# Cross attention and experts on one core: weights transposed by VectorE and moved through DRAM instead of transposed by TensorE

## The chip, the core and the metric

The kernel runs on one core of one Trainium2 chip. TensorE (PE; its weight loads are listed as PEld) multiplies from on-chip memory (SBUF) into accumulators (PSUM[...]); VectorE (DVE), ScalarE (ACT) and GpSimd (POOL) do the rest; SyncE (SP) issues most DMAs between SBUF and the chip's DRAM. The engines run their own instruction lists in order and wait for each other by semaphores. The metric is the device time of one execution in microseconds (us), lower being better.

## The reference

```python
# x (4,1024,256); ctx (4,77,256); fside (4,16); 16 heads of 64
def _L0_xattn_ref(x, latents, shift, scale, ...):
    xn = layernorm(x, ln1_w, ln1_b);  ln = layernorm(latents, ln2_w, ln2_b)
    q = ln @ Wq;  k, v = jnp.split(xn @ Wkv, 2, axis=-1)
    q = q * (1.0 + scale[:, None, :, None]) + shift[:, None, :, None]
    qk = jnp.einsum('bihd,bjhd->bhij', q, k) * DIM_HEAD ** (-0.5)
    out = jnp.einsum('bhij,bjhd->bihd', jax.nn.softmax(qk, axis=-1), v)
    return out.reshape(b, -1, INNER) @ Wout

x = x + _L0_xattn_ref(ctx, _layernorm(x), fside, fside, ...)
x = x + _L0_ffn_ref(_layernorm(x), Wr, Wg, Wu, Wd)   # 9 experts of width 704, top 2, silu gate
```

The call passes the 77 context rows as `x` and the 4,096 tokens as `latents`: each token asks 77 keys in each of 16 heads. The second part routes each token to two of nine experts. All is float32.

## The kernel before

Tokens are taken in 8 groups of 512 (`NG`), and a group in 4 sub-blocks of 128 (`NS`): 32 sub-blocks in all, numbered i. The key, query and output matrices are folded beforehand: `g_sb[b]` gives the scores of a normalised token against all 16 x 77 head-keys of batch b in one product, and `u_sb[b]` takes the 1,232 softmax weights of a token straight to its 256 outputs and 9 router logits (`DE` = 265). A batch has two groups. The weights of 64 keys per head fill 8 chunks of 128 rows, the remaining 13 keys of each head two more: `KC` = 10 chunks.

One sub-block goes through these steps:

- `query` (L241, VectorE) normalises the tokens, `query_turn` (L250, TensorE, then a ScalarE copy) turns them.
- `scores` (L263) makes three PSUM banks of 462, 462 and 317 columns, each with one buffer, and VectorE takes each head's negative maximum (L267).
- `exponentials` (L277) runs one ScalarE instruction per head, 16 in all, into `ex`; `queries_logits` (L288) takes the router's share.
- `attention_weights`: VectorE sums `ex` (L297), inverts (L299), and multiplies into `an` (L301 and L305), which has two buffers.
- `weights_turn` (L313 to L319): TensorE transposes the ten chunks of `an` into three PSUM tiles, so that keys lie on partitions; `weights_copy` (L321 to L327): ScalarE copies these to `aT`.
- `values` (L336): ten products of `aT` with `u_sb` (in the profile two matrix instructions each); `attended` (L344, L345) adds the result to x and to the logits; `residual_stats` (L351) prepares the second norm.

The order is written out by hand in the loop from L1434 (the kernel runs under a manual schedule, so each engine gets its instructions in program order). Iteration i holds the scores and exponentials of sub-block i, and the transposes, copies and values of sub-block i - 1. On TensorE the order is scores, weight transposes, query transposes of i + 1, values. Routing of group g - 1 (second norm, logits, top two, places in the experts' lists) is spread over the same iterations as short VectorE instructions; SP writes `out` (L847) and `y_d` (L881) once per group and loads x two groups ahead (L204).

Ahead of the loop, context products fill `g_sb` and `u_sb`. `fill` (L793) makes parts of `u_sb` (16 parts, batch by chunk pair); the other 13 keys' part, `urem`, is placed in `u_sb` by 32 small SBUF-to-SBUF DMAs (L769).

After the loop come the expert blocks: six "early" ones (256 tokens of one expert), whose lists rest on the first five groups, and then pairs, single units and mixed ones, whose lists need all groups. The routing of the last group and the tables of these late blocks (`late_blocks`, L1054) are handed out by `pump` (L1369), `STEP` = 6 steps after each of a block's six hidden tiles (L1242); when the steps are used up, `fetch` issues on POOL the gathers of the late blocks' row lists (`ids`, L1183) and rows (`yin`, L1183). Block j's `turn` (L1228, TensorE) is put behind block j - 1's hidden tiles; then comes `down` (L1320) of the block before, whose result `adding` (L1355, POOL) adds to the output.

Of the kernel before, what the change touches and what calls it, by code (L numbers as in the profile page):

```python
# [8 lines left out]
F32 = mybir.dt.float32  # L9
# [12 lines left out]
def kernel(  # L22
# [76 lines left out]
    y_d = dram.tile([TOK, D], F32, name="y_d")  # L99
    list_d = dram.tile([ROWS, 2], I32, name="list_d")  # L100
# [88 lines left out]
    def open_attention():  # L189
        for name, bufs in (("xpool", 3), ("qpool", 2), ("rpool", 2)):  # L190
            pools[name] = attention.enter_context(tc.tile_pool(name=name, bufs=bufs, side="right"))
        q = pools["qpool"]
        zs.extend(q.tile([P, D], F32, name=f"z{i}", bufs=1) for i in range(2))
        an_of.extend(q.tile([P, NA], F32, name=f"an{i}", bufs=1) for i in range(2))
        for z in zs:
            nc.gpsimd.memset(z[:, D - 1 : D], 1.0)
        for an in an_of:
            nc.gpsimd.memset(an[:, H * JA :], 0.0)
# [14 lines left out]
    def query_variance(g):  # L213

        st = zstats.pop(g)
        mv = stat.tile([P, NS, 2], F32, tag="mvq", name=f"mv_q{g}", bufs=2)
# [18 lines left out]
    zTs, exs, ans, lgs, aTs, nmx, fstats, pscs = {}, {}, {}, {}, {}, {}, {}, {}  # L235
# [36 lines left out]
    def exponentials(i, k):  # L272
        h, n = banks[k]
        if k == 0:
            exs[i] = pools["qpool"].tile([P, H, J], F32, tag="ex", name=f"ex{i}")
        for q in range(n):
            nc.scalar.activation(  # L277
                exs[i][:, h + q, :], pscs[k][:, q * J : (q + 1) * J], AF.Exp,
                bias=nmx[i][:, h + q : h + q + 1],
            )  # L280
# [12 lines left out]
    def attention_weights(i):  # L293

        ex = exs.pop(i)
        sm = stat.tile([P, H], F32, tag="sm", name=f"sm{i}")
        nc.vector.tensor_reduce(sm, ex, AX.X, ALU.add)  # L297
        rs = stat.tile([P, H], F32, tag="rs", name=f"rs{i}")
        nc.vector.reciprocal(rs, sm)  # L299
        an = ans[i] = an_of[i % 2]  # L300
# [3 lines left out]
        )  # L304
        nc.vector.tensor_tensor(  # L305
            an[:, H * JA :].rearrange("p (h w) -> p h w", w=W)[:, :, :JR], ex[:, :, JA:J],
            rs.unsqueeze(2).to_broadcast([P, H, JR]), ALU.mult,
        )

    TURNS = [(k, min(4, KC - k)) for k in range(0, KC, 4)]  # L310
    pas = {}

    def weights_turn(i):  # L313
        for k, m in TURNS:
            pa = pas[k] = mm_tile(f"pa{i}_{k}")
            for q in range(m):
                nc.tensor.transpose(  # L317
                    pa[:, q * P : (q + 1) * P], ans[i][:, (k + q) * P : (k + q + 1) * P], ident
                )  # L319

    def weights_copy(i, t):  # L321
        if t == 0:
            aTs[i] = pools["qpool"].tile([P, KC, P], F32, tag="aT", name=f"aT{i}")
        k, m = TURNS[t]
        nc.scalar.copy(  # L325
            aTs[i][:, k : k + m, :].rearrange("p k t -> p (k t)"), pas[k][:, : m * P]
        )  # L327

    pos = {}

    def values(i):
        b = i // NS // GPB
        aT = aTs.pop(i)
        po = pos[i] = mm_tile(f"po{i}")
        for n in range(KC):
            nc.tensor.matmul(  # L336
                po[:, :DE], aT[:, n, :], u_sb[b][:, n, :], start=(n == 0), stop=(n == KC - 1)
# [18 lines left out]
    with ExitStack() as kvs:  # L356
# [247 lines left out]
        for i in range(2):  # L604
            nc.gpsimd.memset(u_half[i][:, :, NP:, :], 0.0)
# [158 lines left out]

        def other_keys_placed(b):
            for k in range(2):
                for q in range(2 * N2 // NR):
                    at = (2 * q + k) * W
                    nc.sync.dma_start(  # L769
                        out=u_sb[b][at : at + JR, NP:, :],  # L770
                        in_=urem[64 * k + b * W : 64 * k + b * W + JR].rearrange(
                            "p (r q) d -> p r q d", r=NR
                        )[:, :, q, :],
                    )

        EARLY_V = 5
        QB = TB // P
        for n in range(EARLY_V):
            if n < 2:
                for c in range(C):  # L780
                    turn_wo(n * QB, c)
            elif n == 3:
                wo_logits()
            context_values(n)
            if n == 3:
                for q in range(NS):
                    query_stats(0, q)
                query_variance(0)
                query_root(0)
                query_scale(0)  # L790
        turn_logits()
# [5 lines left out]

        context_values(EARLY_V)
        fill((0, 0), (1, 0), (2, 0), (3, 0), new=bank_tile)

        nc.scalar.activation(junk, eps_t, AF.Exp)
        context_values(EARLY_V + 1)
        fill((0, 1), (1, 1), new=bank_tile)
        context_values(EARLY_V + 2)
        for n in range(N2):
            other_keys(n)
        for b in range(B):
            other_keys_placed(b)
        query(0)
        fill((0, 2), (1, 2))  # L810
        query_turn(0)
        query(1)
        fill((0, 3), (1, 3))
        for k in range(len(banks)):
            scores(0, k)
            exponentials(0, k)
            if k == 0:
                fill((2, 1), (3, 1))
                query_turn(1)
            else:  # L820
                fill((1 + k, 2))
    left = [(2, 3), (3, 3)]
# [322 lines left out]
    def weights(j):  # L1145
# [9 lines left out]
        load(tabs[kind][0][0:1, at : at + 1], w, downs[j][0])  # L1155

    def weights_upper(j):

        _, i, kind = blocks[j]
        if kind == "flex":  # L1160
            load(tabs[kind][0][0:1, 2 * i + 1 : 2 * i + 2], late["w2"], late["d2"])

    def load(number, w, d):
# [5 lines left out]
        nc.sync.dma_start(out=w[:, :, 0:FF], in_=wg_v)  # L1169
        nc.sync.dma_start(out=w[:, :, FF : FF + FT], in_=wu_v[:, :, NF * P :])  # L1170
        nc.sync.dma_start(out=w[:, :, FF + FT : FF + FB], in_=wu_v[:, :, FA : NF * P])
        nc.sync.dma_start(out=w[:, :, FF + FB :], in_=wu_v[:, :, 0:FA])
        nc.sync.dma_start(
# [5 lines left out]
        )  # L1179

# [26 lines left out]

    Q = 32
# [157 lines left out]
    STEP, HOLD = 6, 3  # L1366
# [20 lines left out]
    def fetch():  # L1387

        end = NBLK if late_ready() else EARLY
        for name, fn, lead in (  # L1390
# [8 lines left out]
            while ahead[name] < min(now[0] + lead + 1, end):  # L1399
                fn(ahead[name])  # L1400
# [31 lines left out]
    N_SUB = NG * NS  # L1432
    chosen, early = None, None
    for i in range(N_SUB + 1):  # L1434
        g, s = divmod(i, NS)
        now_on = i < N_SUB
        q = g - 1

        if now_on:
            if i:  # L1440
                scores(i, 0)
                if i < 3:
                    fill(left[i - 1])
                exponentials(i, 0)
            if i > 1:
                residual_stats(i - 2)
            if i:
                scores(i, 1)
            if 0 < i < N_SUB - 1:
                query(i + 1)  # L1450
            if i:
                scores(i, 2)
        if i:
            weights_turn(i - 1)
            weights_copy(i - 1, 0)
            weights_copy(i - 1, 1)
        if i == 2:
            vsides.close()
        if now_on and i:
            exponentials(i, 1)  # L1460
        if 0 < i < N_SUB - 1:
            query_turn(i + 1)
        if now_on and i:
            exponentials(i, 2)
        if i:
            weights_copy(i - 1, 2)
        if now_on:
            queries_logits(i)
            if s == 1 and q > 0:
                ranks(q - 1)  # L1470
            if i == (G_EARLY + 1) * NS + 2:
                early = early_blocks()
                advance(early, 2)
        else:
            turn(0)
            advance(chosen)
            ranks(q - 1)
            residual_stats(i - 2)
        if i:
            values(i - 1)  # L1480


        if now_on and s == 0:
            if g + 1 < NG:
                for k in range(NS):
# [132 lines left out]
```

## Time and profile before

| what | us |
|---|---|
| median of 3 runs (lowest, highest) | 908.5 (907.83, 910.33) |
| the profiled execution's own time | 908.26 |
| its span in the trace | 906.6 |
| TensorE busy in the span | 890.6 (98%) |
| VectorE busy | 588.2 (65%) |
| ScalarE busy | 317.8 (35%) |
| GpSimd busy | 315.9 (35%) |
| preparation, up to the loop's first repeated part | 0 to 75.5 |
| sub-blocks | 75.5 to 388 |
| expert blocks | 388 to 906.6 |

The shares are averages over stages with different limits, so the table is only a start: VectorE's 65% says little about the sub-blocks, where it is busier than among the experts. In the page's groups a row reads: line, engine, operation, result<-operands, shapes, count | busy time in all, mean length of one in ns | idle time of the engine just ahead of it and what ended it. Instructions of one engine overlap, so busy time divided by the count can be well under the mean length. How long a step holds TensorE is read from the starts in the timeline.

The page's chain of waits covers only the last few us, DMAs of the final additions, so it isn't used here. The waits view of TensorE lists 8 causes of waiting, the largest 2.4 us (the first weights' arrival) and none of them repeated.

### The profile page before, as it was taken

What the parts mean: (1) busy time and instruction counts of PE and PEld (TensorE: products, weight loads), DVE (VectorE), ACT (ScalarE), POOL (GpSimd) and SP (SyncE); (2) the same over time, 40 slices, a digit from 0 to 9 for tenths busy, and PEclk for the clock granted to TensorE, in tenths of its full rate; (3) what the DMA queues carried; (4) which work ended last, traced back from release to release, by engine and by line L of the source; (5) the groups of instructions that cost most, each with busy time, mean ns of one, the idle gap of its engine ahead of it and who ended that gap; (6) DMA issues with size and microseconds to landing.
All of it is one profiled execution on the core that took longest, in us unless ns stands there. A gap on an engine that the chain in (4) does not pass through costs nothing. (4 is left out here: it accounts for less than half of the span.)

```text
span 906.6 us, 13816 instructions
## 1 busy us (share of the span) xinstructions
PE 890.6 (98%) x4184; PEld 684.0 (75%) x4184; DVE 588.2 (65%) x1854; ACT 317.8 (35%) x1021; POOL 315.9 (35%) x328
## 2 busy tenths in 40 slices
PE   8999999999999999999999999999999999999996
PEld 6656777777777777788887777777777777778885
DVE  5776688878888887753626666666665666665641
ACT  3566566565656566551211111111111111111110
POOL 3000002130504252146554445435435435444332
PEclk9999999999999999999999999999999999999998
DMA  7011010503202710456769779779879878779722
GB/s 266 3 21 43 24 47 25 47 25 47 66 28 48 227 36 24 120 145 183 184 193 301 214 221 305 221 218 303 242 212 317 229 216 229 221 224 321 235 30 23
DMA packets 110379, 137.94 MB, mean 152 GB/s; under 512 B 24664, under 2 KB 80288, under 8 KB 110305
## 3 DMA queue, kind: packets, MB, share of 16 engines
q1 hardware_dynamic: 92746, 119.66, 43.2%
q0 software_dynamic: 17344, 17.26, 10.1%
q8 instruction: 34, 0.56, 0.3%
q14 instruction: 41, 0.33, 0.2%
q10 hardware_dynamic: 214, 0.13, 0.0%
HBM read 119.48 MB, written 18.33 MB: 152 GB/s over the span
## 5 line engine op out<-in xcount | busy, mean ns | idle before, releaser
L1242 PE MATMUL pg<-xT,wgu 128*128 128x256 f32 x1144 | 251.7, 379 | 0.7 <-DVE xT L1215 0.7
L1242 PEld LDWEIGHTS pg<-xT,wgu 128*128 128x128 f32 x1144 | 215.9, 190 | 29.6 <-issue 1.1
L1320 PE MATMUL po<-wd,hid 128*128 128x256 f32 (+1 forms) x804 | 180.9, 380 | 0.0
L1320 PEld LDWEIGHTS po<-wd,hid 128*128 128x128 f32 (+1 forms) x804 | 149.2, 187 | 28.0 <-issue 3.7
L277 ACT ACTIVATE ex<-psc,mx 128x77 f32<-128x77 f32 x512 | 123.6, 360 | 100.1 <-DVE mx L267 98.8
L1215 DVE STREAM_TRANSPOSE xT<-yin 32x128 f32<-32x128 f32 (+1 forms) x544 | 148.4, 273 | 14.2 <-DMA yin<-y_d,ids 5.4
L1355 POOL DMA_INDIRECT out_dram<-co,ids x63 | 100.7, 1599 | 162.0 <-DVE co L1323 133.9
L950 POOL DMA_INDIRECT list_d<-r_entry,r_pli x64 | 69.0, 1078 | 247.3 <-issue 119.7
L336 PE MATMUL po<-u,aT 128*128 128x265 f32 x640 | 151.7, 391 | 0.5 <-ACT aT L325 0.2
L263 PE MATMUL psc<-g,zT 128*128 128x462 f32 (+1 forms) x384 | 139.7, 511 | 0.0
L336 PEld LDWEIGHTS po<-u,aT 128*128 128x128 f32 x640 | 118.7, 189 | 23.3 <-ACT aT L325 1.5
L1249 DVE TENSOR_TENSOR hid<-pg,sl 128x256 f32<-128x256 f32 x130 | 55.0, 424 | 121.8 <-ACT sl L1248 120.8
L1248 ACT ACTIVATE sl<-pg 128x256 f32<-128x256 f32 x130 | 49.7, 383 | 219.6 <-PE pg L1242 193.0
L263 PEld LDWEIGHTS psc<-g,zT 128*128 128x128 f32 x384 | 72.2, 189 | 58.2 <-issue 50.8
L1183 POOL DMA_INDIRECT yin<-y_d,ids x67 | 70.2, 1048 | 26.5 <-issue 18.9
L297 DVE TENSOR_REDUCE sm<-ex 128x16 f32<-128x1232 f32 x32 | 45.9, 1435 | 35.9 <-ACT ex L277 35.9
L267 DVE TENSOR_REDUCE mx<-psc 128x6 f32<-128x462 f32 (+1 forms) x96 | 55.7, 580 | 19.7 <-PE psc L263 16.9
L1323 DVE TENSOR_SCALAR co<-po,ids 128x256 f32<-128x256 f32 x67 | 32.3, 484 | 53.0 <-PE po L1320 51.4
L325 ACT COPY aT<-pa 128x512 f32<-128x512 f32 (+1 forms) x96 | 49.4, 552 | 27.7 <-PE pa L317 27.7
L317 PEld LDWEIGHTS pa<-ident,an 128*128 128x128 f32 x320 | 36.9, 141 | 7.7 <-PE po L336 1.4
L317 PE MATMUL pa<-ident,an 128*128 128x128 f32 x320 | 40.2, 273 | 1.0 <-DVE an L301 1.0
L301 DVE TENSOR_TENSOR an<-ex,rs 128x1024 f32<-128x1024 f32 x32 | 39.2, 1224 | 1.1
(312 smaller groups left out, 761.2 us busy)
## 6 DMA issues: line engine op xcount, KB each, us to landing
wgu<-in_L_ffn_Wg_dram SPq DMA_DIRECT2D x41, 704.0 KB
wd<-in_L_ffn_Wd_dram SPq DMA_DIRECT2D x41, 640.0 KB
wgu<-in_L_ffn_Wu_dram SPq DMA_DIRECT2D x41, 512.0 KB
wgu<-in_L_ffn_Wu_dram SPq DMA_DIRECT2D x41, 128.0 KB
x<-in_x_dram SPq DMA_DIRECT2D x8, 512.0 KB
out_dram<-x SPq DMA_DIRECT2D x8, 512.0 KB
y_d<-y SPq DMA_DIRECT2D x8, 512.0 KB
w<-in_L_ffn_Wg_dram SPq DMA_DIRECT2D x5, 704.0 KB
```

Of the source, the lines that this page charges most:

```text
L263: nc.tensor.matmul(psc[:, :w], zT[:, c, :], g_sb[i // NS // GPB][:, c, h * J : h * J + w], start=(c == 0), stop=(c == C - 1),)
L267: nc.vector.tensor_reduce(nmx[i][:, h : h + n], psc[:, : n * J].rearrange("p (h j) -> p h j", h=n), AX.X, ALU.max, negate=True,)
L277: nc.scalar.activation(exs[i][:, h + q, :], pscs[k][:, q * J : (q + 1) * J], AF.Exp, bias=nmx[i][:, h + q : h + q + 1],)
L317: nc.tensor.transpose(pa[:, q * P : (q + 1) * P], ans[i][:, (k + q) * P : (k + q + 1) * P], ident)
L336: nc.tensor.matmul(po[:, :DE], aT[:, n, :], u_sb[b][:, n, :], start=(n == 0), stop=(n == KC - 1))
L950: i = nc.gpsimd.indirect_dma_start(out=list_d[:, :], out_offset=bass.IndirectOffsetOnAxis(ap=place_i[:, s : s + 1], axis=0), in_=entries[k ...
L1183: return nc.gpsimd.indirect_dma_start(out=dst, out_offset=None, in_=src, in_offset=bass.IndirectOffsetOnAxis(ap=offsets, axis=0), **kw,)
L1215: yield nc.vector.transpose(xT[q : q + Q].rearrange("p c (h t) -> p h c t", t=P)[:, :nh, :, a : a + Q], of(yins, j)[a : a + Q].rearrange(" ...
L1242: nc.tensor.matmul(pg[:, g, :], w[:, c, at : at + P], xT[:, c, :], start=(c == 0), stop=(c == C - 1),)
L1249: nc.vector.tensor_tensor(hid[:, f, :], pg[:, 1, :], sl, ALU.mult)
L1320: nc.tensor.matmul(po[rows, :D], hid[:, f, at], d[:, f, :], start=(f == 0), stop=(f == NF))
L1355: i = nc.gpsimd.indirect_dma_start(out=out_r, out_offset=bass.IndirectOffsetOnAxis(ap=rows_of(j, h, rows), axis=0), in_=cos[j][:, h, :], i ...
```

## The change

The ten TensorE transposes and three ScalarE copies of each sub-block go. Instead VectorE transposes `an` in squares of 32 by 32 within each quarter of the partitions, one DMA writes the result to DRAM (`a_d`, two buffers), and four DMAs read it back with the keys of each chunk on their partitions. `aT` keeps two buffers; `an` and the transposed `anT` have one. Keys are numbered so that the four quarters fit (the second multiplication writes in another order; `u_sb`'s other keys go through a DRAM tile, `u_d`, in one write and eight reads). The exponentials give out their sums by `accum_out`, and the VectorE sum goes.

```diff
 def exponentials(i, k):
...
-                bias=nmx[i][:, h + q : h + q + 1],
+                bias=nmx[i][:, h + q : h + q + 1], accum_out=sms[i][:, h + q : h + q + 1],
...
 def attention_weights(i):
-        ex = exs.pop(i)
-        sm = stat.tile([P, H], F32, tag="sm", name=f"sm{i}")
-        nc.vector.tensor_reduce(sm, ex, AX.X, ALU.add)
+        ex, sm = exs.pop(i), sms.pop(i)
...
-        an = ans[i] = an_of[i % 2]
+        an = an_of[0]
...
     def weights_turn(i):
-        for k, m in TURNS:
-            pa = pas[k] = mm_tile(f"pa{i}_{k}")
-            for q in range(m):
-                nc.tensor.transpose(
-                    pa[:, q * P : (q + 1) * P], ans[i][:, (k + q) * P : (k + q + 1) * P], ident
-                )
...
-        nc.scalar.copy(
-            aTs[i][:, k : k + m, :].rearrange("p k t -> p (k t)"), pas[k][:, : m * P]
-        )
+        turned = pools["qpool"].tile([P, NQ, Q, KC], F32, tag="anT", name=f"anT{i}", bufs=1)
+        nc.vector.transpose(
+            turned.rearrange("p q t k -> p q k t"), an_of[0].rearrange("p (k q t) -> p q k t", q=NQ, t=Q)
+        )
+        aT = aTs[i] = pools["qpool"].tile([P, NQ, Q * KC], F32, tag="aT", name=f"aT{i}")
+        there = a_d[i % 2]
+        nc.sync.dma_start(out=there, in_=turned.rearrange("p q t k -> p (q t k)"))
+        by_key = there.rearrange("(a i) (q m) -> q i a m", i=Q, q=NQ)
+        for q in range(NQ):
+            nc.sync.dma_start(out=aT[q * Q : (q + 1) * Q], in_=by_key[q])
...
     def values(i):
...
-        aT = aTs.pop(i)
+        aT = aTs.pop(i).rearrange("p a (t k) -> p (a t) k", k=KC)
...
-                po[:, :DE], aT[:, n, :], u_sb[b][:, n, :], start=(n == 0), stop=(n == KC - 1)
+                po[:, :DE], aT[:, :, n], u_sb[b][:, n, :], start=(n == 0), stop=(n == KC - 1)
```

The loop is written anew. Iteration i holds the scores of i, the weights and their transposes of i - 1 and the values of i - 3 (`LAG` = 3); all that follows a group's values moves with them. Scores of sub-block 0 are made among the context products, and 12 of the 16 fills move into iterations 1 to 3. The expert weights of the first three blocks are issued in parts, between the DMAs of `aT`:

```diff
+            attention_weights(i - 1)
...
+            weights_turn(i - 1)
...
+            values(d)
...
-            if advance(early, 7):
+            if advance(early, 9):
                 early = None
                 now[0] = -1
-                fetch()
+                fetch(in_parts=True)
+        elif partly and advance(partly[0], 1):
+            partly.pop(0)
...
+    late_values(N_SUB - 2)
+    rest.append(listed_second_last())
+    in_first = {2: [last_values], 3: [lambda: turn(1)]}
...
-    STEP, HOLD = 6, 3
+    STEP, HOLD = 8, 3
```

The values of the last sub-block are put behind the third hidden tile of the first expert block, and the routing of the last two groups, not of one, is handed out by `pump`, 8 steps at a time. `load_x` keeps four groups in place of three. The other keys' placing:

```diff
+        def other_keys_there():
+            nc.sync.dma_start(out=u_d, in_=urem.rearrange("p n d -> p (n d)"))
...
-                for q in range(2 * N2 // NR):
-                    at = (2 * q + k) * W
-                    nc.sync.dma_start(
-                        out=u_sb[b][at : at + JR, NP:, :],
...
+                nc.sync.dma_start(
+                    out=u_sb[b][64 * k : 64 * k + 64, NP:, :],
+                    in_=rows[k, b].rearrange("p (t d) -> p t d", t=2),
+                )
```

Two memsets of `u_half` on POOL go with it.

## The prediction

> **What bounds the kernel now.** I read the busy times by stage first, then the order of TensorE's work inside one attention sub-block, then the costliest groups. The windows view (columns: length, then busy time and instructions of PE, PEld, DVE, ACT, POOL, then clock, DMA share, GB/s) gives for six groups of four sub-blocks and for the stage after them:
>
> ```profile
> 116.00:362.00 246.00, 245.73 (x1087) 179.75 (x1086) 201.76 (x600) 148.46 (x541) 62.40 (x76) 1.00 0.24 57
> 388.00:490.00 102.00, 101.58 (x482) 88.74 (x481) 50.62 (x201) 26.38 (x55) 55.60 (x54) 1.00 0.73 202
> ```
>
> TensorE has work in 245.7 of 246 us at a granted clock of 1.00: it is the bound. A sub-block lasts 246/24 = 10.25 us; VectorE is busy 201.76/24 = 8.41 of it, ScalarE 6.19. The timeline of TensorE shows what fills one:
>
> ```profile
> 206.64 4.33 PE L263 MATMUL psc<-g,zT 128*128 128x462 f32 x12
> 210.81 1.25 PE L317 MATMUL pa<-ident,an 128*128 128x128 f32 x10
> 211.90 0.38 PE L250 MATMUL pz<-ident,z 128*128 128x128 f32 x2
> 212.14 4.75 PE L336 MATMUL po<-u,aT 128*128 128x265 f32 x20
> ```
>
> From start to start: scores 4.17, weight transposes 1.09, query transposes 0.24, values (to 216.72, the next scores) 4.58. The page's groups price the rest:
>
> ```profile
> L277 ACT ACTIVATE ex<-psc,mx 128x77 f32<-128x77 f32 x512 | 123.6, 360 | 100.1 <-DVE mx L267 98.8
> L336 PEld LDWEIGHTS po<-u,aT 128*128 128x128 f32 x640 | 118.7, 189 | 23.3 <-ACT aT L325 1.5
> L297 DVE TENSOR_REDUCE sm<-ex 128x16 f32<-128x1232 f32 x32 | 45.9, 1435 | 35.9 <-ACT ex L277 35.9
> L325 ACT COPY aT<-pa 128x512 f32<-128x512 f32 (+1 forms) x96 | 49.4, 552 | 27.7 <-PE pa L317 27.7
> ```
>
> **The change, part by part.**
>
> TensorE loses the ten transposes (L317): 10.25 - 1.09 = 9.16 us per sub-block. What is late next? VectorE. Its 8.41 us busy are not all of its time: an instruction that needs the result just ahead starts some 35 ns after it (rs ends at 206.68 in the timeline, an starts at 206.72). About 12 of its 25 instructions per sub-block are such: 0.4 us. So it needs 8.8 of 10.25 now.
>
> VectorE loses the sums (1.435) and gains one transpose of 128x1280 per sub-block, T. The trace has transposes of 32 partitions in two sizes (groups with shapes kept apart):
>
> ```profile
> L1215 DVE STREAM_TRANSPOSE xT<-yin 32x128 f32<-32x128 f32 x304 | 91.9, 302 | 10.4 <-DMA yin<-y_d,ids 5.4 <-DVE co L1323 0.6
> L1215 DVE STREAM_TRANSPOSE xT<-yin 32x64 f32<-32x64 f32 x240 | 56.5, 235 | 3.9
> ```
>
> (302-235)/64 = 1.05 ns an element, 168 ns fixed: T = 168 + 1280 x 1.05 = 1.51 us, an even trade. But those write runs of 32 neighbours; the new one writes single words 40 bytes apart (turned is [q, t, k] with k innermost, written along t). Three reductions, found under the tiles pairs, units and halves, show what a step costs on the reading side:
>
> ```profile
> L1065 DVE TENSOR_REDUCE pairs<-steps x1: 442/442/442, 424.3 to 424.3; 128x9 f32<-128x144 f32 x1
> L1071 DVE TENSOR_REDUCE units<-steps x1: 448/448/448, 435.9 to 435.9; 128x9 f32<-128x288 f32 x1
> L1077 DVE TENSOR_REDUCE halves<-steps x1: 744/744/744, 448.6 to 448.6; 128x9 f32<-128x576 f32 x1
> ```
>
> They read every fourth, every second and every word. 288 and 576 elements give 1.03 ns each and 152 fixed; 144 elements at 16 bytes should then take 300 and take 442: 2.0 ns each. [...] I take 2.69, 6 to 4: nothing makes a write exempt. Then VectorE needs 8.8 - 1.44 + 2.69 = 10.1 us per sub-block, and is the bound in TensorE's place.
>
> The value products' weights, aT[:, :, n], are read 40 bytes apart as well. A load of 128 columns takes 189 ns, one of 64 columns 132 (group pu<-wo_sb,vals, L746): 0.9 ns a column. Products start every 4.58/20 = 229 ns, loads run beside them, and in the transposes loads of 141 ns follow each other every 1.09/10 = 109, so part of a load overlaps the next. Twice the time per column makes the streaming part about 115 x 2 = 230 ns: just hidden. Ends: 0, and 189 + 115 - 229 = 75 ns x 20 = 1.5 us per sub-block. I take 0, 2 to 1.
>
> ScalarE loses the three copies (49.4/32 = 1.54) and its 16 exponentials also give out their sums. No row shows that. Below 0 it cannot go: the same elements still pass. Nearest is a small ScalarE instruction on its own, junk at L1497, 203 ns. An exponential takes 241 ns of the engine (123.6/512) at a length of 360; with no overlap it would add (360-241) + 203 = 0.32. I take 0.2, the small instruction: 6.19 - 1.54 + 16 x 0.2 = 7.85 us, beside 10.1. The upper end gives 9.8.
>
> SP gains five DMAs per sub-block, 655 KB out and 655 KB back, in one queue. An issue of x or out_dram occupies SP some 0.35 us, so five take about 2 of a sub-block's 10. The read waits for its own write and, as aT has two buffers, for the values of three sub-blocks back, which end with the iteration; behind that SP holds the next write, x, y_d and the expert weights (issued in parts for this). Moving 1.3 MB at the 202 GB/s of the later stage takes 6.5 us; landing about 6 us into the next iteration, used 4 us into the one after: 7 us of cover, cost 0. If a landing takes more than that, the excess falls on TensorE in every sub-block. [...] Here each run is 32 x 10 words = 1,280 contiguous bytes, and 80,288 of this trace's 110,379 packets are under 2 KB while slices reach 321 GB/s; I take the trace.
>
> Start. Scores and softmax of sub-block 0 move ahead among the context products, 12 of the 16 fills move into iterations 1 to 3, and values begin in iteration 3. Iterations 1 and 2 hold for TensorE 4.17 + 0.24 + four fills at 0.52 (two took 47.79 to 48.84 in the timeline) = 6.5 us, while ScalarE needs 16 x 0.44 for exponentials and about 2.4 for copies, 9.5, and VectorE 8.4. I take half of the 3 us each as made up by work begun earlier: 3 us lost. The single write and eight reads in place of 32 copies (SP spent 20.9 us on 24 of these) end long before the first values: 0. The dropped memsets were POOL's, idle there: 0.
>
> Handover. The values of the last three sub-blocks follow the scores; those of the second last come 5 us after the release of their buffer, their read needs 6 to 7: 1.5 us lost.
>
> Tables of the late blocks. The routing of one more group now runs in the expert stage, 8 steps a turn in place of 6. Counting steps, the tables end after the first tile of block 5, before in block 4 after the fifth; the built order agrees. POOL therefore queues the row lists of block 6 behind two additions to the output of block 3:
>
> ```profile
> 449.65 1.02 POOL L1183 DMA_INDIRECT ids<-list_d,pair_ai  x1 [0.30 <-issue]
> 453.76 1.05 POOL L1183 DMA_INDIRECT yin<-y_d,ids  x1 [3.09 <-PE pg L1242]
> 458.94 1.62 POOL L1355 DMA_INDIRECT out_dram<-co,ids  x1 [0.30 <-issue]
> 460.87 1.57 POOL L1355 DMA_INDIRECT out_dram<-co,ids  x1 [0.30 <-issue]
> 468.81 0.60 PE L1228 MATMUL px<-ident,yin 128*128 128x128 f32 x4
> ```
>
> On these times: lists issued at 462.7, landed 4.1 later (453.76 - 449.65), two gathers from 467.1, the second issued at 468.5 and landed 4.5 later (the DMA view's median): 473.0, where TensorE wants them at 468.8. 4 us lost; nothing if the tables end one turn earlier than counted.
>
> **The sum**, against the profiled execution (span 906.6, its own time 908.3, the runs' median 908.5): 29 full sub-blocks at 10.25 - 10.1 = 0.15 give -4.4; start +3, handover +1.5, tables +4. 908.3 - 4.4 + 8.5 = **912.4 us**. About 0.3% (2.7 us) is what these runs can tell from no change.
>
> **The rivals.**
>
> A, not slower: VectorE's write at 40 bytes runs at full rate. T = 1.51, VectorE needs 8.9, TensorE bounds at 9.16; VectorE's routing comes in lumps, so 9.35. 29 x 0.90 = 26: 908.3 - 26 + 8.5 = 891. For it: transposes are priced at one word per 1.05 ns, and reads at 8 bytes cost nothing. Against: reads at 16 bytes. It decides from T below 2.54 us, where 29 times the gain exceeds 8.5.
>
> B, the weight load's stride isn't hidden: up to 9.16 + 1.5 = 10.66 us on TensorE: 908.3 + 29 x 0.41 + 8.5 = 929 at most, half of it 918 with VectorE near the same pace. For it: the margin is nil. Against: loads overlap now.
>
> C, the accumulating exponentials bind: at 0.32 each ScalarE needs 9.8, with table loads in lumps behind which the next zT waits, 10.3: 918. Against: two small instructions usually overlap, as the 241 of 360 ns show.
>
> **Chances.** The forecast 0.38, A 0.27, B 0.24, C 0.11. The forecast's own range is 904 to 918, B and C lie over 910, A at 884 to 900. Range 887 to 929. Faster: A, and a quarter of the forecast (T between the ends): 0.35. Same 0.10. Slower 0.55.
>
> **What would show it.** The transpose's mean: 1.5 or 2.7 us. The spacing of the value products: 229 ns or more. In the windows of the attention stage, which engine is never idle, and the sub-block's length against 10.1. A TensorE wait at px for yin of about 4 us before block 6. A small ScalarE instruction beside each exponential, at 0.2 us. I am wrong if T is under 2 us, or if values wait for the DMA of aT.

## The result, and the profile after

The changed kernel takes **914.7 us** (median of 6 runs, 912.9 to 916.5), the kernel before beside it 908.6 (907.8 to 910.3): a ratio of 1.0065, 95% interval 1.0046 to 1.0084. It is slower by 0.65%. The forecast was 912.4. The profiled execution took 913.8 with a span of 912.1, 5.5 us over the span before.

The total is near the forecast, but it isn't made up as the sum said. The windows view of the profile after (columns as before the change) gives 24 sub-blocks and the stretch in which attention ends:

```profile
123.50:362.07 238.57, 226.56 (x842) 174.08 (x841) 212.45 (x581) 152.93 (x844) 57.49 (x72) 0.98 0.62 175
362.07:395.10 33.03, 27.77 (x110) 25.04 (x110) 20.02 (x65) 11.10 (x41) 14.68 (x17) 0.90 0.80 221
```

TensorE stood 0.3 us of 246 in this stage before; now it stands 12.0 us of 238.6, and the granted clock is 0.98 in place of 1.00. VectorE is busy 212.45/24 = 8.85 us per sub-block, 0.44 more than before. The timeline of TensorE in a sub-block without routing:

```profile
123.50 4.84 PE L338 MATMUL po<-u,aT 128*128 128x265 f32 x20
128.18 4.33 PE L265 MATMUL psc<-g,zT 128*128 128x462 f32 x12
132.35 0.38 PE L252 MATMUL pz<-ident,z 128*128 128x128 f32 x2
132.57 1.64 PE L338 MATMUL po<-u,aT 128*128 128x265 f32 x6
```

From values to values it is 132.57 - 123.50 = 9.07 us with no gap: here TensorE is the bound, not VectorE. The first values start at 87.23 and those of sub-block 28 at 362.07: 274.84 us for 28, or 9.82 on average. The same stretch in the kernel before:

```profile
69.28 4.75 PE L336 MATMUL po<-u,aT 128*128 128x265 f32 x20 [0.20 <-ACT aT L325]
355.02 4.73 PE L336 MATMUL po<-u,aT 128*128 128x265 f32 x20
```

That is 285.74 us, or 10.21 on average, 0.39 more. And 274.84 - 28 x 9.07 = **20.9 us** are lost again in some sub-blocks. Which ones? The waits views of TensorE and of VectorE for just these 28 (waiting instruction, what it waited for: us in all, times, longest) name them:

```profile
PE pz L252 <- DVE z L243: 8.8, 7, 2.2
PE psc L265 <- DVE r_o L908: 2.7, 1, 2.7
PE psc L265 <- ACT lg L291: 0.5, 1, 0.5
```

```profile
DVE anT L321 <- DMA a_d<-anT: 10.2, 4, 5.4
DVE mx L269 <- PE psc L265: 6.9, 9, 1.1
DVE bn_q L213 <- DMA x<-in_x_dram: 5.6, 5, 2.1
```

TensorE waits 12.0 us in all, nearly all of it for VectorE. VectorE in turn waits for DMAs: at the transpose, because the only anT is freed when its write to a_d has landed, and at the statistics of x (`bn_q`), because x isn't there yet. A row that names VectorE as the cause isn't the end of the search; one has to ask what VectorE waited for. None of these 28 waits for aT itself.

The largest case, first on GpSimd (the first and last of its eight list scatters: small DMAs that write the tokens' places in the experts' lists, `list_d`), then on SP, then on VectorE and ScalarE, in their timelines:

```profile
166.97 1.10 POOL L957 DMA_INDIRECT list_d<-r_entry,r_pli  x1 [130.75 <-DVE r_pli L955]
...
176.21 0.97 POOL L957 DMA_INDIRECT list_d<-r_entry,r_pli  x1 [0.30 <-issue]
```

```profile
164.05 0.34 SPq L326 DMA_DIRECT2D a_d<-anT  x1
167.05 1.73 SPq L329 DMA_DIRECT2D aT<-a_d  x4
168.82 0.43 SPq L854 DMA_DIRECT2D out_dram<-x  x1
172.97 0.34 SPq L326 DMA_DIRECT2D a_d<-anT  x1
184.68 1.74 SPq L329 DMA_DIRECT2D aT<-a_d  x4
```

```profile
178.69 0.61 DVE L269 TENSOR_REDUCE mx<-psc 128x6 f32<-128x462 f32 x1
184.72 2.44 DVE L321 STREAM_TRANSPOSE anT<-an 128x1280 f32<-128x1280 f32 x1 [5.41 <-DMA a_d<-anT]
188.68 0.28 ACT L291 ACTIVATE lg<-psc,qsd 128x9 f32<-128x9 f32 x1
189.01 2.48 PE L265 MATMUL psc<-g,zT 128*128 128x317 f32 x4 [2.74 <-DVE r_o L908]
```

The reads of aT are issued when the write has landed. The first write takes 167.05 - 164.05 = 3.0 us; the second, issued while GpSimd scatters the routing lists, 11.7. VectorE stands 5.41 us for it, with the maximum of the third bank behind it, then that bank's exponentials and router share (`lg`) on ScalarE, and then TensorE's next scores into this bank. (The `r_o` that the last line names is routing work, which the scores don't use; `lg`, the last reader of the bank, ends at 188.96 too.) TensorE then pays twice, as the windows over the same stretch show (after the length: busy time and instructions of PE, PEld, DVE, ACT, POOL, then clock, DMA share, GB/s):

```profile
184.00:186.00 2.00, 2.00 (x6) 0.75 (x4) 1.28 (x1) 0.00 (x0) 0.00 (x0) 1.00 0.11 22
186.00:188.00 2.00, 0.27 (x1) 0.00 (x0) 1.97 (x5) 0.54 (x4) 0.00 (x0) 1.00 1.02 248
188.00:190.00 2.00, 0.99 (x2) 0.80 (x3) 1.69 (x10) 0.96 (x7) 0.00 (x0) 0.57 1.03 352
190.00:192.00 2.00, 1.49 (x3) 0.38 (x2) 1.90 (x9) 0.16 (x1) 0.00 (x0) 0.50 0.71 296
```

After the gap of 2.74 us the granted clock is 0.57 and 0.50. The values that follow take 5.78 us from start to start in place of 4.68, and these two sub-blocks together 25.87 (178.34 to 204.21) in place of 18.14: 7.7 more, of which 4.2 are TensorE's waits (2.74, 0.63 and 0.86), 0.4 two small products of the routing and 3.1 slower products. Of the 20.9 us in all, 12.0 are waits. The routing's small products add 6 x 0.36 = 2.2, which the kernel before had as well. In windows of half a microsecond the clock is at half in two stretches only, from about 188.3 to 195.1 and from 246.2 to 249.8, which cost some 4.6. The last 2 us were not followed.

The groups of the page on the exponentials, the weight load and the transpose (line engine op, count | busy, mean ns | idle ahead):

```profile
L280 ACT ACTIVATE ex<-psc,mx 128x77 f32<-128x77 f32 x512 | 158.8, 332 | 103.1 <-DVE mx L269 100.2
L338 PEld LDWEIGHTS po<-u,aT 128*128 128x128 f32 x640 | 151.6, 313 | 8.7 <-issue 5.9
L280 ACT ACTIVATION_READ_ACCUMULATOR ex<-psc,mx 128x1 f32 x512 | 108.3, 212 | 0.0
L321 DVE STREAM_TRANSPOSE anT<-an 128x1280 f32<-128x1280 f32 x32 | 79.5, 2486 | 11.4 <-DMA a_d<-anT 11.3
```

The transpose takes 2.49 us, (2486 - 168)/1280 = 1.81 ns a word. Each exponential has a small companion of 212 ns, and the load of the values' weights takes 313 ns in place of 189.

The end of attention, in TensorE's timeline:

```profile
362.07 4.93 PE L338 MATMUL po<-u,aT 128*128 128x265 f32 x20
369.91 7.75 PE L338 MATMUL po<-u,aT 128*128 128x265 f32 x20 [2.90 <-DMA aT<-a_d]
377.49 0.60 PE L1243 MATMUL px<-ident,yin 128*128 128x128 f32 x4
377.93 4.87 PE L338 MATMUL po<-u,aT 128*128 128x265 f32 x20
382.63 5.34 PE L1257 MATMUL pg<-xT,wgu 128*128 128x256 f32 x24
390.34 4.93 PE L338 MATMUL po<-u,aT 128*128 128x265 f32 x20 [2.36 <-DMA aT<-a_d]
395.10 1.24 PE L1257 MATMUL pg<-xT,wgu 128*128 128x256 f32 x5
```

Two waits for aT, 2.90 and 2.36 us; the second values run 7.75 us in place of 4.87, again at half the clock. What did the reads of these two aT wait for? SP's timeline, for sub-blocks 29 and 31:

```profile
358.89 0.52 SPq L326 DMA_DIRECT2D a_d<-anT  x1
364.75 1.74 SPq L329 DMA_DIRECT2D aT<-a_d  x4
374.61 0.45 SPq L326 DMA_DIRECT2D a_d<-anT  x1
385.19 1.74 SPq L329 DMA_DIRECT2D aT<-a_d  x4
```

The values start 5.2 us after the reads are issued, both times. The buffers had long been free: the values of 27 end at 357.7 and those of 29 at 377.7. What came last was the landing of their own writes, 5.9 and 10.6 us after the issue, and SP's waits view says the same (`SPq L329 <- DMA a_d<-anT: 24.2, 4, 10.1` from 355 to 392, and no other row for the reads).

**The account** of the 5.5 us, from the one profile of each kernel:

- Start, +9.6. When the first values start, at 87.23, the scores of four sub-blocks are done. The kernel before stood at its first values at 69.28 with two; two more (8.34), two query transposes (0.48) and a fill (0.61), less the weight transposes already made (1.09), bring it to 77.6. 1.6 of the 9.6 are lost before the output weights' transposes (at 35.02, before at 33.45), where little was changed. In the thirteen profiles of this change and its variants, the first values start between 83.6 and 87.8.
- 28 sub-blocks, -10.0: 285.74 without the fill and a query transpose that moved, against 274.84.
- Handover, +8.1: the two waits 5.3, values at half the clock 2.9.
- Late tables, +2.5: from the last values to block 6's first product, the block 0 products that moved ahead of the last values counted in. TensorE waits 2.3 for `yin` there.
- Behind that, +0.7.
- Outside the 28 sub-blocks, -5.4: four times the weight transposes (4.4), and a wait of 1.0 for `an` at the end.

### The profile page after: what moved, and what is told of

Same layout as the page of the kernel before. It is cut to its first block, busy times and chain, and to the rows that moved or that the text cites. A ratio compares the mean times of both kernels' runs of the same rounds, so it can differ in the third digit from the quotient of the medians.

```text
span 912.1 us, 13776 instructions
## 1 busy us (share of the span) xinstructions
PE 873.2 (96%) x3864; PEld 680.0 (75%) x3864; DVE 611.2 (67%) x1854; ACT 326.6 (36%) x1437; POOL 311.5 (34%) x325
## 5 line engine op out<-in xcount | busy, mean ns | idle before, releaser
L280 ACT ACTIVATE ex<-psc,mx 128x77 f32<-128x77 f32 x512 | 158.8, 332 | 103.1 <-DVE mx L269 100.2
L338 PE MATMUL po<-u,aT 128*128 128x265 f32 x640 | 161.4, 409 | 5.3 <-DMA aT<-a_d 5.3
L338 PEld LDWEIGHTS po<-u,aT 128*128 128x128 f32 x640 | 151.6, 313 | 8.7 <-issue 5.9
L957 POOL DMA_INDIRECT list_d<-r_entry,r_pli x64 | 64.4, 1006 | 271.7 <-DVE r_pli L955 154.7
L265 PE MATMUL psc<-g,zT 128*128 128x462 f32 (+1 forms) x384 | 142.6, 517 | 5.0 <-DVE r_o L908 2.7
L280 ACT ACTIVATION_READ_ACCUMULATOR ex<-psc,mx 128x1 f32 x512 | 108.3, 212 | 0.0
L321 DVE STREAM_TRANSPOSE anT<-an 128x1280 f32<-128x1280 f32 x32 | 79.5, 2486 | 11.4 <-DMA a_d<-anT 11.3
L269 DVE TENSOR_REDUCE mx<-psc 128x6 f32<-128x462 f32 (+1 forms) x96 | 53.4, 556 | 15.0 <-PE psc L265 15.0
L1323 ACT COPY hid<-ph 128x384 f32<-128x384 f32 x15 | 7.2, 479 | 78.4 <-PE ph L1318 78.4
L1299 ACT ACTIVATE hs<-psg 128x512 f32<-128x512 f32 x15 | 9.0, 597 | 65.3 <-PE psg L1295 65.3
```

Source lines behind the costliest of these rows:

```text
L265: nc.tensor.matmul(psc[:, :w], zT[:, c, :], g_sb[i // NS // GPB][:, c, h * J : h * J + w], start=(c == 0), stop=(c == C - 1),)
L269: nc.vector.tensor_reduce(nmx[i][:, h : h + n], psc[:, : n * J].rearrange("p (h j) -> p h j", h=n), AX.X, ALU.max, negate=True,)
L280: nc.scalar.activation(exs[i][:, h + q, :], pscs[k][:, q * J : (q + 1) * J], AF.Exp, bias=nmx[i][:, h + q : h + q + 1], accum_out=sms[i][: ...
L321: nc.vector.transpose(turned.rearrange("p q t k -> p q k t"), an_of[0].rearrange("p (k q t) -> p q k t", q=NQ, t=Q))
L338: nc.tensor.matmul(po[:, :DE], aT[:, :, n], u_sb[b][:, n, :], start=(n == 0), stop=(n == KC - 1))
L957: i = nc.gpsimd.indirect_dma_start(out=list_d[:, :], out_offset=bass.IndirectOffsetOnAxis(ap=place_i[:, s : s + 1], axis=0), in_=entries[k ...
```

## The experiments

The sub-blocks column is the time from the first values to those of sub-block 28 in the run's one profile; the other columns are of all its executions. In turn_contiguous and load_contiguous the values multiply weights of other keys, so each was timed in a single execution and only its attention stage is read. The runs were made in four sets, each on a chip of its own with the kernel before beside it: anT_two to sums_back, scatter_spread to tables_earlier, after_again to stats_later_aT3, and all_three. So small differences count within a set, less across sets.

| kernel | 28 sub-blocks | median us (range) | ratio to before, 95% |
|---|---|---|---|
| changed | 274.8 | 914.7 (912.9 to 916.5) | 1.0065 (1.0046 to 1.0084) |
| anT_two | 272.2 | 909.2 (903.8 to 916.2) | 0.9995 (0.9979 to 1.0012) |
| turn_contiguous | 266.9 | 905.0, a single execution | |
| aT_three | 273.4 | 907.1 (905.4 to 913.4) | 0.9989 (0.9968 to 1.0010) |
| sums_back | 295.2 | 931.1 (930.3 to 932.4) | 1.0238 (1.0219 to 1.0257) |
| scatter_spread | 278.5 | 916.1 (912.0 to 923.3) | 1.0069 (1.0041 to 1.0096) |
| scatter_spread_aT3 | 274.6 | 915.9 (911.2 to 921.1) | 1.0058 (1.0030 to 1.0085) |
| load_contiguous | 273.1 | 911.2, a single execution | |
| tables_earlier | 274.5 | 909.5 (905.8 to 917.6) | 0.9991 (0.9975 to 1.0007) |
| after_again | 274.4 | 914.9 (911.2 to 917.1) | 1.0058 (1.0036 to 1.0080) |
| stats_later | 266.0 | 903.7 (900.4 to 908.7) | 0.9927 (0.9905 to 0.9949) |
| stats_later_aT3 | 266.1 | 901.9 (898.4 to 905.4) | 0.9911 (0.9887 to 0.9935) |
| all_three | 273.8 | 906.1 (903.2 to 912.1) | 0.9954 (0.9936 to 0.9971) |

### A second anT

```diff
-name=f"anT{i}", bufs=1)
+name=f"anT{i}", bufs=2)
```

> The changed kernel, with two buffers of anT in place of one. What is seen after the change: sub-blocks without routing take 9.07 us from values to values, 28 of them together 20.9 us more than 28 x 9.07, and VectorE stands 11.3 us in all at its transposes until the write of the one before has landed in a_d. Landing theory (the single anT makes VectorE wait for a DMA that lands late): VectorE's 11.3 us of waiting are gone, the excess of 20.9 falls to 12 or less, the total to about 905. Length theory (VectorE's own work is too long, as the prediction has it): the waits go but the excess stays near 19 and the total within 2 us of 914. If the late landing only moves on to aT, values wait for aT in the same sub-blocks, some 5 us in all, and the total is about 910.

VectorE's waits at the transpose are gone, but the 28 sub-blocks are only 2.6 us shorter, and 18.2 of the 20.9 us remain. The waits views of TensorE and of VectorE for these 28:

```profile
PE pz L252 <- DVE z L243: 10.1, 5, 4.9
PE po L338 <- DMA aT<-a_d: 1.1, 1, 1.1
```

```profile
DVE bn_q L213 <- DMA x<-in_x_dram: 10.8, 5, 6.4
DVE mx L269 <- PE psc L265: 6.3, 9, 1.1
```

The late landing moves on, but not to aT as the third case of the expectation has it: values wait for it 1.1 us here (the 8.9 of the whole profile are nearly all at the end of attention). It moves on to x, loaded behind the reads of aT in the same queue: VectorE now waits 10.8 us for it, in place of 5.6. Neither theory had this. The median lies 5.5 us under that of the changed kernel; the profiled executions differ by 1.3, so most of that fall isn't explained.

### The transpose with a contiguous write

```diff
-tile([P, NQ, Q, KC], F32, tag="anT", name=f"anT{i}", bufs=1)
+tile([P, NQ, KC, Q], F32, tag="anT", name=f"anT{i}", bufs=1)
...
-turned.rearrange("p q t k -> p q k t"), an_of[0].rearrange(
+turned, an_of[0].rearrange(
...
-nc.sync.dma_start(out=there, in_=turned.rearrange("p q t k -> p (q t k)"))
+nc.sync.dma_start(out=there, in_=turned.rearrange("p q k t -> p (q k t)"))
```

> The changed kernel with anT laid out so that the transpose writes runs of 32 neighbouring words, all else the same; the values then multiply weights of other keys, so only the attention stage up to 362 us is compared. Both theories: the transpose takes 1.5 us in place of 2.49 if the 40-byte step of the write is what it pays for. Length theory: each of the sub-blocks with routing is up to 1 us shorter, the excess of 20.9 us over 28 x 9.07 falls to 5 or less. Landing theory: the waits for a_d stay near 11 us and the excess falls only by 3 to 7 us.

The tile view of anT (ns min/median/max):

```profile
L321 DVE STREAM_TRANSPOSE anT<-an x32: 1490/1503/1516, 62.4 to 364.5; 128x1280 f32<-128x1280 f32 x32
```

1.50 us: the step of 40 bytes alone makes the other 0.98. The excess over 28 x 9.07 falls from 20.9 to 12.9. That is more than the landing theory allowed (7 at most, it is 8.0) and far less than the length theory wanted (to 5 or less). So the length counts, but how much isn't shown: in the same 28 sub-blocks VectorE's waits for the write fell from 10.2 to 4.3 us, those for x rose from 5.6 to 9.7, and this is one execution.

### The sums back on VectorE

```diff
-bias=nmx[i][:, h + q : h + q + 1], accum_out=sms[i][:, h + q : h + q + 1],
+bias=nmx[i][:, h + q : h + q + 1],
...
         ex, sm = exs.pop(i), sms.pop(i)
+        nc.vector.tensor_reduce(sm, ex, AX.X, ALU.add)
```

> The changed kernel with the sums on VectorE again and the exponentials without a sum. Length theory: VectorE gains 1.435 us in every one of 29 sub-blocks, it is the bound at about 10.1 and goes to 11.5: total about 914 + 35 = 950. Landing theory: TensorE bounds the sub-blocks without routing (9.07 stays within 0.2), and only those with routing, about half, take 1.4 more: total 925 to 935. ScalarE theory (the exponentials with sums are what holds): 0.30 us an exponential goes back to 0.21 and the total falls.

931.1 us, as the landing theory had it. 28 sub-blocks cost 20.4 us more, where 28 x 1.435 = 40 would be due if VectorE bound them all. The first four, which have no routing, stay at 9.07 with or without the exponentials' sums: there ScalarE holds nothing up. In the sub-blocks with routing VectorE's added work could hide a gain on ScalarE; none is seen.

### Three aT

```diff
-name=f"aT{i}")
+name=f"aT{i}", bufs=3)
```

> The changed kernel with three buffers of aT in place of two. Handover theory (the read of the last aT waits for the values of three sub-blocks back): TensorE's two waits for aT of 5.3 us at the end of attention go, and with them the values that ran at half the clock (2.9 us): total 907 to 910. Rival (the DMA itself is late there, behind the expert weights in the same queue): the waits stay within 1.5 us of 5.3 and the total within 2 us of 914.5.

The median falls by 7.6 us, within the first theory's range, but not by its mechanism. From the values of sub-block 28 to the last ones it takes 27.52 us here and 28.27 in the changed kernel: 0.75 less. The first wait is still there, 3.35 us, with values of 7.48 at half the clock behind it. The second is put down to another engine (1.44 us, `hid`), but the last values again start 5.1 us after the reads of their aT are issued, and these again were issued when the write had landed, 9.4 us after its issue. The third buffer frees what nobody was waiting for. Of the 6.7 us between the two profiled executions, 3.5 are the start, though nothing there was changed (first values at 83.74; x landed earlier and the output weights' copy on ScalarE didn't wait), 1.4 the 28 sub-blocks and 1.0 lie behind the last values. Why the median falls stays open.

### The scatters spread

```diff
-                advance(places(q - 1))
+                placing = places(q - 1, parts=True)
+                advance(placing, 7)
+        if gr >= 0 and sr == 2 and q > 0:
+            advance(placing, 6)
...
+        if gr >= 0 and sr == 3 and q > 0:
+            advance(placing)
```

> The changed kernel, with the eight list scatters of a group (list_d, on GpSimd's queue) issued three, three and two in consecutive sub-blocks in place of eight in one stretch of 10 us. In the traces so far the write of anT to a_d lands 3.0 us after its issue when no scatter is under way and 5 to 12 us after it when one is. Scatter theory (the scatters hold up the landing): no landing over 7 us, the longest waits of VectorE for a_d go, the 28 sub-blocks are 10 us or more shorter than in the changed kernel, the total 903 to 907. Rival (the 512 KB transfers of x, y_d and out hold it up): landings in the same sub-blocks stay at 5 to 12 us and the total stays at 910 to 915.

> The scatters spread and three buffers of aT together. Scatter theory: both gains add, since one is in the middle of attention and one at its end: total 899 to 904, faster than the kernel before. Rival (the same late landing lies behind both, so that the gains overlap): no better than the better of the two alone by more than 2 us.

Both miss. Landings up to 9.3 and 10.8 us remain and the totals are those of the changed kernel, 916. The edit did less than meant: GpSimd issued the first group's scatters from 167 to 178 us, in place of 167 to 176, with 2.8 us from the start of the fourth to that of the fifth. The premise was too strong as well: writes with no scatter under way had taken up to 8.0 us in the traces so far (anT_two, at 346). What these profiles do show is another wait. In the timeline of VectorE with the scatters spread, before the longest sub-block of 14.6 us ends:

```profile
242.28 1.41 DVE L213 BATCH_NORM_STATS2 bn_q<-x 128x6 f32<-128x256 f32 x4 [4.13 <-DMA x<-in_x_dram]
```

SP issued this x at 236.81, behind reads of aT that had waited for a late write. That led to the last runs but one.

### Contiguous weights for the values

```diff
-aT = aTs.pop(i).rearrange("p a (t k) -> p (a t) k", k=KC)
+aT = aTs.pop(i).rearrange("p a m -> p (a m)").rearrange("p (k t) -> p t k", k=KC)
```

> The changed kernel with the values' weights read as runs of 128 neighbouring words in place of words 40 bytes apart; the values then multiply weights of other keys, so only the attention stage is compared. If the step of 40 bytes is what the load pays for: LDWEIGHTS of the values 189 ns in place of 313. Hidden theory (the prediction's): values from start to start stay within 0.1 us of the 4.68 seen for 20 products, sub-blocks without routing at 9.07 become 8.97 at best. Rival B (the load sets the pace): values fall to 4.4 or less.

The load's tile view:

```profile
L338 PEld LDWEIGHTS po<-u,aT x640: 186/190/338, 83.5 to 392.6; 128*128 128x128 f32 x160
```

190 ns, and 20 products in 4.48 us in place of 4.68, 8.87 in place of 9.07 per sub-block. So the step isn't quite hidden: 0.20 us a sub-block, twice what the hidden theory gave, an eighth of rival B's upper end. Of the 28 x 0.20 = 5.6 us only 1.8 are seen in the 28 sub-blocks; that VectorE sets the pace of the others is the likely reason, not shown.

### The late tables earlier

```diff
-    STEP, HOLD = 8, 3
+    STEP, HOLD = 12, 3
```

> The changed kernel with 12 steps of the late tables after each hidden tile in place of 8. Late-tables theory (the prediction's): TensorE's wait for yin before block 6 (2.3 us, and 2.8 us of time from attention's end to block 6's first product) goes, total 2 to 4 us lower. Rival: longer bursts of VectorE steps between hidden tiles hold TensorE elsewhere in blocks 0 to 4, and the time from attention's end to block 6 does not fall.

The wait for `yin` is gone from TensorE's waits, and the median is 5.2 us lower. In the profiles the way from the end of the last values to block 6's first product is 82.6 us, and was 83.9: 1.3 less, for 2.3 us of waits that went. So both theories have a share here, and the rest of the median's fall isn't explained.

### The statistics of x later

```diff
-        if s == 2 and g + 2 < NG:
+        if s == 3 and g + 2 < NG:
             for k in range(NS):
                 query_stats(g + 2, k)
```

> The changed kernel once more, unaltered, beside the next two on one chip, since the total of kernels with the transfers over DRAM has been seen to vary by some 10 us from execution to execution. If that spread is the landings' and not the edits', this one spreads over 905 to 917 as well, with a median of 910 to 915.

> The changed kernel with the statistics of a group's x taken one sub-block later, just ahead of their use. In the traces VectorE stands at them (bn_q) until x has landed, 10.8 us in all and up to 4.1 at once: x is loaded only one sub-block ahead, in the one queue behind the reads of aT, which wait for the write to a_d. Second-queue theory: these waits fall below 4 us, the 28 sub-blocks are 4 to 8 us shorter than in the changed kernel, total 4 to 7 us below the unaltered kernel beside it. Rival (VectorE's own length in the sub-blocks with routing is what counts; its waits only fill time that it has): total within 2 us of the unaltered one.

> The later statistics and three buffers of aT together. If both waits count: 5 to 10 us below the unaltered changed kernel beside it, and not slower than the kernel before. Rival: no more than 3 us below it.

The unaltered kernel repeats itself, 914.9 us. Moving four instructions of VectorE per group, 1.41 us together, by one sub-block takes 11.3 us off, more than either theory expected; the three aT take 1.8 more, which is well within the two intervals. This is **faster than the kernel before**, by 0.7% and 0.9%. VectorE's waits in the 28 sub-blocks, statistics later:

```profile
DVE mx L269 <- PE psc L265: 7.0, 10, 1.1
DVE x L346 <- PE po L338: 4.6, 4, 1.2
DVE anT L321 <- DMA a_d<-anT: 3.7, 3, 2.2
```

No wait for x is left among them, and that for the write is 3.7 in place of 10.2, with landings as late as before in part (8.6 us at 173, 7.5 at 212). TensorE's waits there are 6.5 in place of 12.0, and the excess over 28 x 9.07 is 12.0 in place of 20.9. The sub-block from 192.60 on, which held a wait of 2.06 us for x, took 11.61 us; its counterpart, from 188.93 on, takes 9.44; 1.1 us of the difference are values at half the clock, which the gap before them had brought. Not told apart: how much of the gain is the wait for x, and how much that 1.41 us of work left a crowded sub-block for another.

### All three

The edits of stats_later, aT_three and tables_earlier in one kernel.

> The later statistics, three buffers of aT and 12 steps of the late tables a turn, together. With the later statistics and three buffers alone, 901.9 us were measured, and TensorE still waits 4.4 us for yin before block 6 there. If the three act in different places: these 4.4 us go, total 896 to 899, ratio to the kernel before about 0.987. Rival (longer bursts of table steps hold the first expert blocks as much): 901 to 903.

906.1 us: 3.6 under the kernel before, but 4 over the same without the earlier tables. The wait for `yin` is gone here too. The profiled executions speak against the rival: from the last values to block 6's first product it takes 87.67 us, and 93.24 without the earlier tables, so these 5.6 are gained; what is lost lies in attention, where the 28 sub-blocks take 7.7 us more. This execution, the longest of its twelve, has the worst landing seen, 12.9 us, and VectorE waits 12.2 us for writes. Why writes land later here isn't settled: the two kernels never ran side by side on one chip. What these runs support keeping is the later statistics; that three aT or earlier tables add to them isn't shown by the medians.

## Why the prediction was right in its total, step by step

The total was right by luck more than by mechanism. With the transpose at its measured 2.49 us in place of 2.69, the same sum gives VectorE 9.85 us per sub-block and a total of 905, under the time before. What brought the total back up are losses that the sum had at nothing or too small.

- **The transpose, 2.69 us: near.** No run shows 2.69: it was an estimate of mine for the write, and the rows of before that show a step (pairs, units, halves) show it for reads alone. What the runs showed in its place is 2.49 with words 40 bytes apart, 1.81 ns a word beside the 2.0 of the read rows, and 1.50 with a contiguous write, where the first of my two ends said 1.51.
- **"VectorE needs 10.1 us per sub-block, and is the bound": wrong as put.** I added VectorE's mean work, routing and all, and made it the length of each sub-block. Its busy time is 8.85, some 9.3 with the 0.4 that the sum sets down for starts behind a result. Without routing TensorE bounds at 9.07 (predicted 9.16). With routing VectorE's list and its waits exceed that. The mean, 9.82, is near 10.1 for another reason, and the gain of these 28 is 10.0 in place of 4.4. The 10.25 was read too high as well: the window from 116 to 362 holds a little over 24 sub-blocks, and from the values of sub-block 5 (120.45) to those of 29 (365.09) it is 10.19. The sum also left out that the second multiplication writes in another order: 536 ns in place of 369 (L307 after, L305 before).
- **"7 us of cover, cost 0": wrong.** The cover was counted for the values alone, and for them it holds until the end of attention. Two other waits hang on the same queue: VectorE for its own write, as anT has one buffer, and VectorE for x, loaded behind the reads of aT. I named both, "one buffer" in the change and "behind that SP holds the next write, x", and put no price on who waits for them. I also took one landing time for all writes; it is 3.0 us at best and up to 11.7 where the list scatters are under way (12.9 in all_three). The price is part of the 20.9 us, of which moving the statistics alone gave back 8.9 in the profile. Runs of 1,280 bytes are written and read here: 3.0 us for the write at best, and values that wait for their reads start 5.1 to 5.2 us after the issue.
- **Start, +3: too small.** 9.6, of which 1.6 come before what the change reorders. I took half of the shortage in the first iterations as made up by earlier work. It wasn't: TensorE waits 6.1 us there for ScalarE and VectorE, 1.7 of it for a copy of output weights that stands on ScalarE behind the root of x's variance, which the new order puts ahead of it.
- **Handover, +1.5: too small, and for another cause.** The sum had the read waiting for the release of its buffer. Both reads were issued 7 us and more after that release, when their own writes had landed, 5.9 and 10.6 us after the issue; and a third buffer left the waits there. It is the one landing time for all writes again. Behind the first of the two waits (5.3 us together) the half clock costs 2.9 more, which the sum didn't know.
- **Tables, +4: about right.** +2.5, and a wait of 2.3 for `yin` where it was placed.
- **ScalarE, no bound: right.** The small companion exists, 212 ns, but it overlaps: 0.300 us from one exponential to the next, 0.207 before. 0.09 each, not 0.2.
- **Rivals.** A fell, though the transpose lies just under the 2.54 us from which A was to decide: the losses took the gain. B fell in size: 0.20 us of its 1.5. C fell: without routing the sub-blocks keep 9.07 with and without the sums.

So 4.4 forecast as gain and 8.5 as loss became some 15.4 (with the 5.4 outside the 28 sub-blocks) and 20.9. The errors nearly cancel, and the total is no proof of the steps.

## What to carry over

The one anT, which a DMA empties, made VectorE wait up to 5.4 us for the landing, so count every instruction that stands behind such a landing, on every engine and in the issuing queue, and not only the consumer. Compare an engine's work with the period sub-block by sub-block, since a mean hides the few in which it decides. Where a load is only one step ahead in a queue that now holds waits, use it a step later: four moved instructions were worth more here (11.3 us of the median) than either added buffer (5.5 and 7.6). Before adding a buffer, look at what its reader waits for: the third aT and the second anT both removed a limit behind which the same late landing stood.

## What the hardware did that I had not expected

The write that took 11.7 us had moved its bytes long before. The DMA view for 174 to 186 us, in 40 slices of 0.3 us:

```profile
GB/s 222 188 35 137 205 188 240 119 103 102 86 86 87 19 55 37 72 1 0 0 0 0 0 0 0 0 0 0 0 0 0 0 0 0 0 0 0 0 26 124
```

Nothing moves after 179.4, yet the landing is seen at 184.7. The three scatters issued in this time land late too, as the same view says (KB left out, median us to landing):

```profile
list_d<-r_entry,r_pli POOLq DMA_INDIRECT x3, 10.1
```

Over the whole profile the scatters' median is 6.7 us, before the change 3.7.

Every write to a_d that took over 8.1 us, in all thirteen traces, was issued with scatters under way; but writes of up to 8.0 us are seen some 10 us behind the last scatter too, beside the larger transfers. That is an association; that the scatters are the cause wasn't shown, as the attempt to spread them hardly did so.

The granted clock fell to 0.5 for 6.8 us around the gaps of TensorE of 2.74 and 2.90 us, some 2 us after each had begun, and for 3.6 us after one of 2.22, when TensorE was already at work again; it stayed at 1.00 after one of 2.36. So the length of a gap alone doesn't say it. At the end of attention a wait of 2.90 us cost as much again in slower values, 7.75 in place of 4.87. The kernel before had no such gap in attention and kept its clock at 1.00.
